# Second layer of a one-core decoder kernel: other exchange of block halves, a shared product in its own output bank, v read from PSUM

## The chip, the cores and the metric

The kernel runs on one core of one Trainium2 chip. The metric is the device time of one execution in microseconds; several executions are taken and the median is given. The profile is of one further execution of the same program.

## The reference, cut to what matters

The decoder has three parts on an input of 16 x 256 x 512 float32: a state-space layer, a gated long convolution along the last axis, and a feed-forward layer with low-rank experts. Each ends in a layer norm with a residual. The change concerns the second part, for head h (32 heads of 8 channels):

```
kv  = v[b,h,i,:] * x2[b,h,j,:]              # all 8 x 8 pairs of channels, 512 positions
y   = causal convolution of kv with k[h]     # the reference uses an FFT of twice the length
y   = y + kv * skip
out[b,h,j,:] = sum over i of y[..i,j,:] * x1[b,h,i,:]
x   = layernorm(x + out)
```

`v` is the output of the first layer; `x1` and `x2` are both the context tensor. The feed-forward part (`base = x @ W.T`, gates from the top two of eight logits, low-rank update) runs in the same loop over heads, one head late.

## The kernel before, in words

The first layer takes the first 757 us of the span. After it comes the loop over 32 heads (line 1198 on). In a head the 512 positions are four blocks of 128, so a Toeplitz matrix of k[h] acts on each pair of blocks (`lb` out, `mb` in). Lag matrices `T` are prepared on the host and loaded by `load_T` into the same buffer as `kv` (two buffers). The 16 batches are two halves, `q` = 0 and 1; in each half `kv` of a block is 128 positions x 512 columns.

For one half of one head the kernel does the following.

- **Products (`products`, L158, VectorE):** `kv` of half q, two instructions of 128x1024, from `vT` and `cT`. They are made one head ahead. `vT` is v with positions on partitions: `turned_v` (L146) makes four TensorE transposes into a PSUM tile of tag `tr`, and ScalarE copies that tile to SBUF (L148).
- **Seed (`seeded`, L1002 and L1003):** blocks 2 and 3 need the same lag matrix on blocks 0 and 1, so GpSimd makes `xs`, the sum of the two (`pair_sum`, L979), TensorE multiplies it once into a PSUM bank of its own (`yc`, in pool `ps_b`), and one ScalarE copy of 128x1024 spreads it over both banks of `y[1]`.
- **Convolution (`convolve`, L1014 and L1032):** four full matmuls of 128x128 on 512 columns (two with differences `Td` of lag matrices, made on GpSimd, L984) and twelve matmuls of 64x64 for the triangles on the diagonal, in three groups of four that run side by side on the four quarters of the array. [...]The result lies in `y[0]` and `y[1]`, two PSUM banks each, with one buffer per tag. The order of blocks and the exchange of 64-row halves (`BLOCKS_IN`, `SWAPPED_IN`, `BLOCKS_OUT`, `SWAPPED_OUT`) are chosen so that the four quarters are taken in every group; one of the quadrants (`AGAIN`) needs a copy of half of `kv` on the other partitions, `kvd`, which ScalarE makes (`again`, L994).
- **Contraction (`multiplied` L1067, `reduced` L1077, VectorE):** each of `y[1]`, `y[0]` is multiplied by `cT` and summed over i, in this order, two instructions of each.

After half 0, the GpSimd part (`skip_term`, then `with_residual`, L948 and L950) adds skip term and v into `o`: one 128x128 instruction and two of 64x384 that move data between partition halves. In half 1 of the contraction the head before is finished: `o + red` on GpSimd (L1225), four transposes (L1104, `centre`), gates (`gates`), the feed-forward matmuls (`feed_forward`, L1193, and `lora`, L1189), and the output.

The engines' order is written by hand: program order is the order on each engine, and the tile framework adds only the waits for data and for buffers. In a head h > 0, TensorE's order is: feed-forward block 3 of the head before, transpose `xat`, seed 0, `lora`, four transposes of v (`turned_v`), convolution 0, four transposes of `centre`, seed 1 (inside `meanwhile`), eight passes for `gl`, feed-forward blocks 0 to 2, convolution 1. VectorE's order is: contraction of half 1 of the head before, row sums, products 0 of the next head, contraction of half 0, products 1 of the next head, gates.

[...]two for tag `tr`, one for `yc`, one for `base`, four for `y`.

Of the kernel before, what the change touches and what calls it, by code (L numbers as in the profile page):

```python
# [37 lines left out]
BLOCKS_IN, SWAPPED_IN = (2, 0, 1, 3), (3,)  # L38
BLOCKS_OUT, SWAPPED_OUT = (0, 1, 3, 2), (0, 1)


GIVEN = ((3, 2), (3, 0), (2, 0), (1, 0), (0, 0), (2, 2), (3, 3))
FULL_AT = {(3, 2): 0, (2, 1): 0, (3, 0): 1, (2, 0): 2, (3, 1): 2, (1, 0): 3}
TRIANGLE_AT = (4, 4, 5, 6)
# [3 lines left out]
    (0, 0, 0), (3, 0, 1), (1, 1, 0), (2, 1, 1),  # L48
    (2, 0, 0), (0, 0, 1), (3, 1, 0), (2, 0, 1),
    (1, 0, 0), (1, 0, 1), (0, 1, 0), (3, 1, 1),  # L50
)

AGAIN = (2, 0, 1)
# [18 lines left out]
def decoder_kernel(  # L72
# [48 lines left out]
    def load_T(h):  # L121

        both = big.tile([P, NQ * NL * BQ * NH * NH + len(GIVEN) * P], F32, tag="big", name="kv")
        kv, T = both[:, 0 : NQ * NL * BQ * NH * NH], both[:, NQ * NL * BQ * NH * NH :]
        T = T.rearrange("p (k l) -> p k l", l=P)
        nc.sync.dma_start(T, toep[h])
        return kv.rearrange("p (q k b j i) -> p q (k b) j i", q=NQ, k=NL, j=NH, i=NH), T

    def load_c(h):


        cT = q3.tile([P, NQ, 7, BQ * NH], F32, tag="cT", name="cT")
        nc.sync.dma_start(cT, ctxT[h])
        return cT
# [7 lines left out]
    def turned_v(vn):  # L142

        tr = ps_t.tile([P, NL, P], F32, tag="tr", name="tr")
        for k, blk in enumerate(BLOCKS_IN):
            nc.tensor.transpose(tr[:, k, :], vn[:, blk * P : (blk + 1) * P], ident)  # L146
        vT = q2.tile([P, NQ, NL, BQ * NH], F32, tag="vT", name="vT")
        nc.scalar.copy(  # L148
            vT.rearrange("p q k t -> p k q t"), tr.rearrange("p k (q t) -> p k q t", q=NQ)
        )  # L150
        return vT

    def products(vT, cT, kv, q, ks=(0, NL // 2)):

        full = [P, NL * BQ // 2, NH, NH]
        for k in ks:
            blks = slice(k, k + NL // 2)
            last = nc.vector.tensor_tensor(  # L158
                kv[:, q, k * BQ : (k + NL // 2) * BQ],
                vT[:, q, blks].rearrange("p k (b i) -> p (k b) i", i=NH).unsqueeze(2)  # L160
                .to_broadcast(full),
                cT[:, q, 1 + k : 1 + k + NL // 2].rearrange("p k (b j) -> p (k b) j", j=NH).unsqueeze(3)
                .to_broadcast(full),
                ALU.mult,
            )
        return last
# [14 lines left out]
    with ExitStack() as s1:  # L181
# [361 lines left out]
        for g in range(NG):  # L543
# [307 lines left out]
            else:  # L851
                finish_sums()
                gated(1, spread_heads(1))
                for n, t in enumerate((0, 2, 1, 3)):


                    ps = ps_s.tile([P, 512], F32, tag="s", name="s") if n in (0, 3) else bank()
                    for c in range(NI):
                        for j in range(2):
                            nc.tensor.matmul(  # L860
                                ps[:, j * S : (j + 1) * S],
                                zs[c][:, t * P : (t + 1) * P],
                                w_o[c // HC, j][c % HC],
                                start=(c == 0 and j == 0),
                                stop=(c == NI - 1),
                                skip_group_check=True,
                            )
                        if n == 3 and c == 3:
                            heads["vT"] = turned_v(heads["vn"].pop(0))
                            heads["vn"] = [load_v(1)]  # L870
                    if n == 3:
                        for q in range(NQ):
                            products(heads["vT"], cTs[0], kvs[0][0], q)
                    r = xs[t]
                    nc.vector.scalar_tensor_tensor(r, r, 2.0, ps, ALU.mult, ALU.add)
                    normalised(g, (t, r))
                    if n == 1:
                        heads["vn"] = [load_v(0)]
                        kvs = [load_T(0), load_T(1)]
# [22 lines left out]
    with ExitStack() as s2:  # L902
# [42 lines left out]
        def with_residual(t, vT):  # L945

            o = p2.tile([P, NQ, NL, BQ * NH], F32, tag="o", name="o")
            nc.gpsimd.tensor_tensor(o[:, :, 3], t[:, :, 0], vT[:, :, 0], ALU.add)  # L948
            for a, b in ((0, HP), (HP, 0)):
                nc.gpsimd.tensor_tensor(  # L950
                    o[b : b + HP, :, 0:3],
                    t[a : a + HP, :, 1:4],
                    vT[a : a + HP, :, 1:4],
                    ALU.add,
                )
            return o
# [15 lines left out]
        def prepared(kv, T):  # L972


            xs = p2.tile([P, NQ, BQ * NH * NH], F32, tag="xs", name="xs")
            Td = p2.tile([P, 2, P], F32, tag="Td", name="Td")

            def pair_sum(q):
                return nc.gpsimd.tensor_tensor(  # L979
                    xs[:, q], moving(kv, q, 0), moving(kv, q, 1), ALU.add  # L980
                )

            def differences():
                nc.gpsimd.tensor_tensor(  # L984
                    Td, T[:, 0:2], T[:, 2:3].to_broadcast([P, 2, P]), ALU.subtract
                )

            return xs, Td, pair_sum, differences

        def again(kv):  # L990

            kvd = p2.tile([P, NQ, BQ * NH * NH], F32, tag="kvd", name="kvd")
            for q in range(NQ):
                nc.scalar.copy(kvd[HP:, q], moving(kv, q, 2)[0:HP])  # L994
            return kvd

        def seeded(y, T, xs, q):

            yc = ps_b.tile([P, BQ * NH * NH], F32, tag="yc", name="yc")
            nc.tensor.matmul(yc, T[:, 2, :], xs[:, q], start=True, stop=True)  # L1002
            nc.scalar.copy(y[1], yc.unsqueeze(1).to_broadcast([P, 2, BQ * NH * NH]))  # L1003

        def convolve(y, kv, T, Td, kvd, q, between=None, late=False, early=None, ahead=None):
# [18 lines left out]
            def quadrant(lb, r, c):  # L1024
                start = lb not in begun and (lb, c) not in begun
                begun.add((lb, c))
                src, at = moving(kv, q, lb), TRIANGLE_AT[lb]
                if (lb, r, c) == AGAIN:

                    r, src, at = 1 - r, kvd[:, q], TRIANGLE_AT[3]  # L1030
                rows, cols = slice(r * HP, (r + 1) * HP), slice(c * HP, (c + 1) * HP)
                return nc.tensor.matmul(  # L1032
                    bank_of(y, lb)[cols],
                    T[rows, at, cols],
                    src[rows],
# [29 lines left out]
        def multiplied(y, cT, q, i):  # L1065
# [4 lines left out]
                cT[:, q, 5 - 5 * i : 7 - 5 * i].rearrange("p k (b i) -> p k b i", i=NH)  # L1070
# [88 lines left out]
        vT_next, vns = heads["vT"], heads["vn"]  # L1159
        more_next = prepared(*kvs[0])  # L1160
        kvd_next = again(kvs[0][0])
# [5 lines left out]
        def ahead():  # L1167
            vT_ahead.append(turned_v(vns.pop(0)))
            vns.append(load_v(2))
            cTs.append(load_c(2))  # L1170
# [10 lines left out]
        def turned_gates(xa, at=None):  # L1181
            xat = (at or ps_t).tile([ER, P], F32, tag="yc" if at else "tr", name="xat")
# [15 lines left out]
        for h in range(HX):  # L1198
            nxt, ff = h + 1 < HX, last is not None
            (kv, T), cT, vT = kvs.pop(0), cTs.pop(0), vT_next  # L1200
            (xs, Td, _, _), kvd = more_next, kvd_next
# [5 lines left out]
            if h:  # L1207
                if rest is not None:
                    base, o_r, xa = rest
                    feed_forward(base, o_r, (3,))  # L1210
                    turned = turned_gates(xa)
# [3 lines left out]
                if nxt:  # L1215
                    vT_after = turned_v(vns.pop(0))
                    kvs.append(load_T(h + 1))
                    if h + 2 < HX:
                        vns.append(load_v(h + 2))
                        cTs.append(load_c(h + 2))  # L1220
# [12 lines left out]
            convolve(y, kv, T, Td, kvd, 0, late=h == 0, ahead=ahead)  # L1233
            if h == 0:
                vT_after = vT_ahead[0]
            ws = skip_sum(sk_next)
            behind = None
            if nxt:
                kv_n, T_n = kvs[0]
                cT_n, vT_next = cTs[0], vT_after  # L1240
                if h:
                    behind = products(vT_next, cT_n, kv_n, 0)
# [4 lines left out]
            else:  # L1247

                prs = []
                for i in range(2):  # L1250
                    prs.append(multiplied(y, cT, 0, i))
                    behind = products(vT_next, cT_n, kv_n, 0, (i * NL // 2,))
# [24 lines left out]
            if nxt:  # L1277
                products(vT_next, cT_n, kv_n, 1)
# [7 lines left out]
            if nxt:  # L1286
                convolve(y, kv, T, Td, kvd, 1)
                kvd_next = again(kv_n)
                rest = (base, o_l, xa) if ff else None
            else:  # L1290
# [3 lines left out]
                    y, kv, T, Td, kvd, 1, lambda: lora(base, turned), True,  # L1294
# [9 lines left out]
        gl = ps_b.tile([P, NE + ER], F32, tag="yc", name="gl")  # L1304
        o_l = {}

        def contracted(src, ks):
# [4 lines left out]
            cs = 5 if ks[0] < 2 else -2  # L1312
# [26 lines left out]
        def norms_and_gates(*ks):  # L1339
            for k in ks:  # L1340
                nc.tensor.transpose(tr[:, k, :], own(k), ident)
            for k in ks:
                nc.tensor.matmul(
                    gl, own(k), w_gl[:, k, :], start=(k == 0), stop=(k == 2),
# [12 lines left out]
        contracted(y_f[2].unsqueeze(1), (3,))  # L1357
        contracted(y_f[1][:, 0:1, :], (2,))
        norms_and_gates(0, 1)
        feed(0)  # L1360
        norms_and_gates(3, 2)
        for k in (1, 3, 2):
            feed(k)
# [84 lines left out]
```

## Time and profile before

| what | value |
|---|---|
| median of 3 runs | 1430.14 us (1429.83 to 1431.35) |
| span of the profiled execution | 1429.6 us |
| granted TensorE clock, mean | 0.999 |
| TensorE busy | 1415.0 us, 99% of the span |
| VectorE busy | 1215.5 us, 85% |
| GpSimd busy | 559.8 us, 39% |
| ScalarE busy | 461.5 us, 32% |
| distance from head to head in the loop | 20.61 us |

The span goes from the first to the last instruction of the core; the profile does not give the time around it. Busy times are unions over instructions of the engine. A line "L1014" is a line of the kernel's source; PE is TensorE's matmul, PEld its weight load, DVE VectorE, ACT ScalarE, POOL GpSimd, SPq the queue that issues DMAs. In a timeline a row is a run of like instructions: start, length, engine, line, operation, output <- inputs, count, and in brackets the idle time before it with what ended it.

### The profile page before, as it was taken

To read this page: it belongs to the slowest core of one execution; us is meant where nothing else is said; L and a number is where in the kernel's file an instruction comes from. 1 tells how busy PE (TensorE), PEld (TensorE's weight loads), DVE (VectorE), ACT (ScalarE), POOL (GpSimd) and SP (SyncE) were. 2 spreads that over 40 slices of the span, in tenths; PEclk is the share of its full clock that TensorE was granted. 3 is DMA by queue.
4 is the path that set the end of the run, shared out by engine and by line. 5 is a ranking of instruction groups with operands and counts; after the bars stand their busy time and mean duration, and the time that the engine had idled before them with its cause. 6 is when DMAs were issued, how large, how long until landed. Compare 5 with 4: busy or idle time off the path is not lost.

```text
span 1429.6 us, 19152 instructions
## 1 busy us (share of the span) xinstructions
PE 1415.0 (99%) x6956; PEld 913.5 (64%) x6956; DVE 1215.5 (85%) x2102; ACT 461.5 (32%) x964; POOL 559.8 (39%) x655
## 2 busy tenths in 40 slices
PE   8999999999999999999999999999999999999997
PEld 7888788787888888888884444444444444444443
DVE  6988778877888787877848999999999999999996
ACT  2423323233232332322312333333333333333331
POOL 5450010100100201001004776677677767766772
PEclk9999999999999999999999999999999999999999
DMA  8014021120121201212003212221221222122200
GB/s 300 33 38 131 16 75 46 38 83 8 56 68 42 74 17 39 83 45 88 15 18 114 71 53 81 74 67 64 82 74 61 69 74 81 60 70 74 80 30 23
DMA packets 49167, 93.38 MB, mean 65 GB/s; under 512 B 8880, under 2 KB 13360, under 8 KB 49072
## 3 DMA queue, kind: packets, MB, share of 16 engines
q1 hardware_dynamic: 49072, 92.15, 20.0%
q8 instruction: 55, 0.90, 0.3%
q14 instruction: 40, 0.33, 0.1%
HBM read 74.82 MB, written 17.32 MB: 64 GB/s over the span
## 4 chain that ended last, share of the span: by engine, by line
PE 96%; DVE 1%; issue 1%; POOL 1%; DMA 0%; SPq 0%; POOLq 0%; ACT 0%; DVEq 0%; ACTq 0%
PE mm L329 20%; PE y L1014 15%; PE s L329 14%; PE y L1032 12%; PE base L1193 8%; PE s L769 6%; PE mm L769 6%; PE yc L1002 4%; PE gl L1270 2%; PE base L1189 2%; PE tr L1104 1%; PE mm L726 1%; PE xm L589 1%; PE mm L860 1%; PE tr L146 1%
## 5 line engine op out<-in xcount | busy, mean ns | idle before, releaser
L1067 DVE TENSOR_TENSOR pr<-y,cT 128x1024 f32<-128x1024 f32 x126 | 148.4, 1219 | 40.4 <-PE y L1032 37.2
L158 DVE TENSOR_TENSOR kv<-vT,cT 128x1024 f32<-128x1024 f32 x128 | 179.4, 1442 | 1.5 <-ACT vT L148 1.5
L1032 PE MATMUL y<-kv 64*64 64x512 f32 x1408 | 179.7, 598 | 0.0
L578 DVE SCALAR_TENSOR_TENSOR acc<-xi,wc,acc 128x512 f32<-128x512 f32 x192 | 142.3, 754 | 7.4 <-ACT acc L574 1.7
L1077 DVE TENSOR_REDUCE red<-pr 128x128 f32<-128x1024 f32 x126 | 147.1, 1208 | 0.0
L1014 PE MATMUL y<-kv 128*128 128x512 f32 x272 | 127.9, 593 | 1.0 <-ACT y L1003 1.0
L1032 PEld LDWEIGHTS y<-kv 64*64 64x64 f32 x1408 | 51.2, 132 | 119.4 <-issue 91.0
L950 POOL TENSOR_TENSOR o<-t,vT 64x384 f32<-64x384 f32 x64 | 121.9, 1905 | 4.4
L1193 PE MATMUL base<-w_f,ol 128*128 128x512 f32 x248 | 119.5, 605 | 0.0
L1014 PE MATMUL y<-kv,Td 128*128 128x512 f32 x248 | 116.5, 592 | 0.0
L67 POOL TENSOR_TENSOR rs_a<-ve_a,nhalf 128x1 f32<-128x1 f32 x32 | 19.0, 594 | 243.1 <-DVE ve_a L65 243.1
L390 POOL TENSOR_TENSOR rstd<-ms,nhalf 128x4 f32<-128x4 f32 (+1 forms) x9 | 8.5, 947 | 260.6 <-DVE ms L388 260.6
L329 PE MATMUL mm<-XT,w_z 128*128 128x256 f32 x384 | 90.7, 379 | 0.0
L1014 PEld LDWEIGHTS y<-kv,Td 128*128 128x128 f32 x248 | 47.1, 190 | 59.3 <-issue 59.3
L979 POOL TENSOR_TENSOR xs<-kv 128x512 f32<-128x512 f32 x63 | 81.3, 1290 | 2.4
L1014 PEld LDWEIGHTS y<-kv 128*128 128x128 f32 x272 | 48.9, 190 | 51.9 <-issue 48.7
L329 PEld LDWEIGHTS mm<-XT,w_z 128*128 128x128 f32 x384 | 73.0, 190 | 9.9
L1193 PEld LDWEIGHTS base<-w_f,ol 128*128 128x128 f32 x248 | 42.3, 189 | 54.5 <-issue 54.5
L1003 ACT COPY y<-yc 128x1024 f32<-128x1024 f32 x62 | 61.8, 997 | 32.9 <-PE yc L1002 23.9
L329 PE MATMUL mm<-xnT,w_z 128*128 128x256 f32 x288 | 71.0, 382 | 0.0
L1225 POOL TENSOR_TENSOR ol<-o,red 128x512 f32<-128x512 f32 x31 | 39.4, 1271 | 79.3 <-DVE red L1077 79.1
L1032 PE MATMUL y<-kvd,kv 64*64 64x512 f32 x128 | 65.2, 589 | 0.0
(278 smaller groups left out, 2940.3 us busy)
## 6 DMA issues: line engine op xcount, KB each, us to landing
cT<-in_ctxT SPq DMA_DIRECT2D x32, 448.0 KB
kv<-in_toep SPq DMA_DIRECT2D x32, 448.0 KB
xt<-in_x SPq DMA_DIRECT2D x32, 256.0 KB
spread<-both SPq DMA_DIRECT2D x32, 256.0 KB
first<-xt SPq DMA_DIRECT2D x32, 256.0 KB
vn<-first SPq DMA_DIRECT2D x32, 256.0 KB
out<-res SPq DMA_DIRECT2D x31, 256.0 KB
xnT<-in_xT SPq DMA_DIRECT2D x7, 1024.0 KB
```

What stands on the lines that cost most here:

```text
L158: last = nc.vector.tensor_tensor(kv[:, q, k * BQ : (k + NL // 2) * BQ], vT[:, q, blks].rearrange("p k (b i) -> p (k b) i", i=NH).unsqueeze ...
L329: nc.tensor.matmul(ps, w[:, p, a, kc, :], Xs[b][:, kc, :], start=start and kc == 0, stop=stop and kc == 1, skip_group_check=upon,)
L578: ins = nc.vector.scalar_tensor_tensor(acc, xi[:, :, k : k + S], wc[:, c, k : k + 1], acc, ALU.mult, ALU.add)
L769: nc.tensor.matmul(ps, own[a][c][:, n * P : (n + 1) * P], w_o[b][c], start=start and c == 0, stop=stop and c == HC - 1, skip_group_check=upon,
L950: nc.gpsimd.tensor_tensor(o[b : b + HP, :, 0:3], t[a : a + HP, :, 1:4], vT[a : a + HP, :, 1:4], ALU.add,)
L979: return nc.gpsimd.tensor_tensor(xs[:, q], moving(kv, q, 0), moving(kv, q, 1), ALU.add)
L1003: nc.scalar.copy(y[1], yc.unsqueeze(1).to_broadcast([P, 2, BQ * NH * NH]))
L1014: nc.tensor.matmul(bank_of(y, lb), w, moving(kv, q, mb), start=not late and lb not in begun, stop=False, skip_group_check=True,)
L1032: return nc.tensor.matmul(bank_of(y, lb)[cols], T[rows, at, cols], src[rows], start=start, stop=False, skip_group_check=True,)
L1067: nc.vector.tensor_tensor(pr.rearrange("p (k b j) i -> p k b j i", k=2, j=NH), y[i].rearrange("p k (b j i) -> p k b j i", j=NH, i=NH), cT[ ...
L1077: nc.vector.tensor_reduce(red[:, q, 2 * i : 2 * i + 2, :].rearrange("p k t -> p (k t)"), pr, AX.X, ALU.add)
L1193: nc.tensor.matmul(base, o_l[:, kc, :], w_f[:, kc, :], start=(first and kc == kcs[0]), stop=False)
```

## The change

Only the second layer is touched.

- The order of blocks and the exchanged halves are others: in (0, 1, 3, 2) with 2 and 3 exchanged, out (1, 0, 2, 3) with 1 and 2 exchanged. With these, all twelve quadrants take `kv` where it lies; `kvd` and its two ScalarE copies a head go. The same number of full matmuls and quadrants is issued.
- `seeded` multiplies straight into the bank of block 3, the second bank of `y[1]`, and two ScalarE copies of 64x512 bring it, halves exchanged, to the bank of block 2. The bank `yc` goes; its place in `ps_b` is a tile of tag `vp`.
- `turned_v` writes the transposes of v to `vp`, already in the order of `vT`. `products` read v from this PSUM tile, and each waits for ScalarE's copy to `vT` as well; `vT` is still made for `with_residual`. In the loop the block with `turned_v`, `load_T`, `load_v` and `load_c` is moved to the head's beginning, ahead of feed-forward block 3, `xat` and the seed.
- `with_residual` takes the two middle blocks and the two outer ones apart: one GpSimd instruction of 128x256 on aligned partitions and two of 64x256 that change halves.
- The host makes six lag matrices and six context blocks a head instead of seven each.

```diff
-BLOCKS_IN, SWAPPED_IN = (2, 0, 1, 3), (3,)
-BLOCKS_OUT, SWAPPED_OUT = (0, 1, 3, 2), (0, 1)
+BLOCKS_IN, SWAPPED_IN = (0, 1, 3, 2), (2, 3)
+BLOCKS_OUT, SWAPPED_OUT = (1, 0, 2, 3), (1, 2)
...
-    def turned_v(vn):
+    def turned_v(vn, pool, tag):
...
-        tr = ps_t.tile([P, NL, P], F32, tag="tr", name="tr")
+        tr = pool.tile([P, NQ, NL, BQ * NH], F32, tag=tag, name="tr")
...
-        return vT
+        kept = nc.scalar.copy(vT, tr)
+        return vT, tr, kept
...
+            if kept is not None:
+                wait_for(last, kept)
...
-            nc.gpsimd.tensor_tensor(o[:, :, 3], t[:, :, 0], vT[:, :, 0], ALU.add)
+            straight, turned = slice(1, 3), slice(0, NL, NL - 1)
+            nc.gpsimd.tensor_tensor(
+                o[:, :, straight], t[:, :, turned], vT[:, :, turned], ALU.add
+            )
             for a, b in ((0, HP), (HP, 0)):
                 nc.gpsimd.tensor_tensor(
-                    o[b : b + HP, :, 0:3],
-                    t[a : a + HP, :, 1:4],
-                    vT[a : a + HP, :, 1:4],
+                    o[b : b + HP, :, turned],
+                    t[a : a + HP, :, straight],
+                    vT[a : a + HP, :, straight],
...
-        def again(kv):
-
-            kvd = p2.tile([P, NQ, BQ * NH * NH], F32, tag="kvd", name="kvd")
-            for q in range(NQ):
-                nc.scalar.copy(kvd[HP:, q], moving(kv, q, 2)[0:HP])
-            return kvd
...
-            yc = ps_b.tile([P, BQ * NH * NH], F32, tag="yc", name="yc")
-            nc.tensor.matmul(yc, T[:, 2, :], xs[:, q], start=True, stop=True)
-            nc.scalar.copy(y[1], yc.unsqueeze(1).to_broadcast([P, 2, BQ * NH * NH]))
+            yc = bank_of(y, 3)
+            nc.tensor.matmul(yc, T[:, SHARED_AT, :], xs[:, q], start=True, stop=True)
+            for a, b in ((0, HP), (HP, 0)):
+                nc.scalar.copy(bank_of(y, 2)[b : b + HP], yc[a : a + HP])
...
             if h:
+                if nxt:
+                    v_after = turned_v(vns.pop(0), ps_b, "vp")
+                    kvs.append(load_T(h + 1))
+                    if h + 2 < HX:
+                        vns.append(load_v(h + 2))
+                        cTs.append(load_c(h + 2))
                 if rest is not None:
...
-                if nxt:
-                    vT_after = turned_v(vns.pop(0))
-                    kvs.append(load_T(h + 1))
-                    if h + 2 < HX:
-                        vns.append(load_v(h + 2))
-                        cTs.append(load_c(h + 2))
...
-                products(vT_next, cT_n, kv_n, 1)
+                products(v_n, cT_n, kv_n, 1)
...
-                convolve(y, kv, T, Td, kvd, 1)
-                kvd_next = again(kv_n)
+                convolve(y, kv, T, Td, 1)
```

## The prediction on record

> **What bounds the kernel now.** I read the page's busy times and chain first, then the sums over the loop of heads (800 to 1400 us), then one head's timeline on TensorE, VectorE and ScalarE, and the waits last.
>
> ```profile
> PE 1415.0 (99%) x6956; PEld 913.5 (64%) x6956; DVE 1215.5 (85%) x2102; ACT 461.5 (32%) x964; POOL 559.8 (39%) x655
> PE 96%; DVE 1%; issue 1%; POOL 1%; DMA 0%; SPq 0%; POOLq 0%; ACT 0%; DVEq 0%; ACTq 0%
> 800.00:1400.00 600.00, 600.00 (x2767) 259.32 (x2769) 554.85 (x726) 216.56 (x466) 418.22 (x468) 1.00 0.21 68
> ```
>
> The third line is the sums: of 600 us PE is busy 600.00 and DVE 554.85. In the timelines (1000 to 1045 us for PE, 1000 to 1024 for DVE and ACT) no PE row carries an idle time:
>
> ```profile
> 1009.12 1.04 PE L1032 MATMUL y<-kv 64*64 64x512 f32 x8
> 1010.08 0.66 PE L1104 MATMUL tr<-ident,ol 128*128 128x128 f32 x4
> 1010.58 1.02 PE L1002 MATMUL yc<-xs,kv 128*128 128x512 f32 x2
> 1011.44 1.09 PE L1270 MATMUL gl<-w_gl,ol 128*128 128x136 f32 x8
> ...
> 1021.20 1.12 PE L1193 MATMUL base<-w_f,ol 128*128 128x512 f32 x2
> 1022.16 0.27 PE L1183 MATMUL xat<-ident,xa 128*128 128x128 f32 x1
> 1022.27 1.02 PE L1002 MATMUL yc<-xs,kv 128*128 128x512 f32 x2
> 1023.13 1.02 PE L1189 MATMUL base<-w_lb,xaT 128*128 128x512 f32 x2
> 1023.99 0.60 PE L146 MATMUL tr<-ident,vn 128*128 128x128 f32 x4
> 1024.43 1.88 PE L1014 MATMUL y<-kv 128*128 128x512 f32 x4
> ```
>
> ```profile
> 1010.25 2.35 DVE L1067 TENSOR_TENSOR pr<-y,cT 128x1024 f32<-128x1024 f32 x2 [1.26 <-PE y L1032]
> ...
> 1021.37 2.35 DVE L1067 TENSOR_TENSOR pr<-y,cT 128x1024 f32<-128x1024 f32 x2
> ```
>
> ```profile
> 1011.68 1.00 ACT L1003 COPY y<-yc 128x1024 f32<-128x1024 f32 x1 [0.16 <-PE yc L1002]
> ```
>
> Passes of 512 columns follow each other every 0.43 us; heads follow every 20.61 us (v's transposes at 1003.38 and 1023.99). DVE waits for PE at half 0's contraction (1.26 us here). So PE sets the time, and a head gets longer by what PE is made to wait and by nothing else. What matters in these rows: the seed (L1002) is what PE does between a convolution and its next work while DVE is still reading the finished `y`. It may do so because its output `yc` is a bank of its own. Only ACT's copy has to wait for DVE.
>
> [...]So a seed written into `y[1]` has to wait for DVE's last read of it. The trace agrees as far as it can: ACT's copy into `y[1]` never overlaps that read (1011.68, after 1011.47).
> [...]POOL's one-column nm_c (L1090) averages 1177 ns where nm_b, the same operation elsewhere, takes 223; the product of 128x1024 averages 1441 ns, and `pr<-y,cT` of equal size, with y in PSUM, 1219.
> [...]Here a gap of 1.36 us left passes at 0.43 us; I count no loss of clock.
>
> **The change, part by part (one head).**
>
> *PE's work:* full matmuls, seeds and the twelve quadrants are as many as before. Each new group of four still takes four different quarters of the array. 0.
>
> *Seed 1, the step that decides.* Convolution 0 ends at 1010.15 (last pass 1009.56 plus 0.59). DVE's first multiplication, that of `y[1]`, starts at 1010.25 and takes 1.22: it ends at 1011.47. From DVE's end to a PE weight load that waited for it the tail shows 0.11 us (xa ends 1421.39, xat's load 1421.505). So seed 1 can begin at 1011.58 in place of 1010.58: 1.01 us. A matmul that waited also starts without its weights loaded ahead: two passes after a wait span 1.13 where others span 1.02 (below), 0.11 more. Together **1.11 us**. Queued behind it on PE are `gl`, three feed-forward blocks and convolution 1, nothing that could go first; the transposes of `centre` are already ahead of it. 30 heads (1 to 30) have it: 30 x 1.11 = **33.4 us**.
>
> *Seed 0 and the moved block.* v's four transposes come first now, so the new order after convolution 1 is: transposes 1021.20 to 1021.69 (as L1104: 0.16, then 0.11 each), feed-forward block 3 to 1022.55, xat to 1022.66, seed. DVE ends with `y[1]` at 1021.37 + 1.22 = 1022.59, plus 0.11 makes 1022.70. The wait is 0.04, the load 0.11: **0.15 us**, in heads 2 to 30: 4.4 us. The moved transposes are thus cover for the seed; without them it would stand 0.43 + 0.11. Head 31 has none to move: 0.5 us. Of what moves with them, SP's three DMAs (T, v, c) are issued sooner; `load_c` must wait until DVE has read the context of the head before (to 1023.7), and behind it on SP is nothing before the output's store, ten us on. `load_T` waits for the end of the convolution as before. ACT makes `vT` ahead of `xaT`, in time that it spends waiting: xaT is ready at about 1023.1, `lora` wants it at 1023.5. The bank `vp` was last read by products 1, which end at 1017.9; it's free. No cost.
>
> *The seed's copies.* Before: one of 997 ns. After: two of 64x512. No row shows that form from PSUM; the nearest are 586 ns (vT, 128x512 from PSUM) and 614 (kvd, 64x512 from SBUF). I take two of 0.59 with starts 0.53 apart, 1.12 us. At seed 0 they run from 1023.91 to 1025.03, and full matmul (3,2), first to need them, loads its weights at about 1025.0 to 1025.2, behind `lora` and full (1,0). It just fits: 0, with bounds of 0 and 0.3 us (9 us in all). At seed 1 there are over 3 us to spare.
>
> *ACT:* kvd's copies (2 x 614 ns) go; ACT is busy 36% in the loop, and its copies end before anything waits. 0. In half 1 the squares for `rs_b` start 1.3 us later, behind the copies; `rs_b` is then ready at about 1015.6, and DVE wants it at 1017.2. Hidden.
>
> *DVE and POOL:* products 1 overlap POOL's `o` and took 3.15 us for two where products 0 took 2.44. Reading v from PSUM should make all four 1.22: 0.7 to 0.9 us a head. The added wait for `kept` ends at about 1022.6, four us before products 0 start. POOL's `o` of 0.46 + 3.96 becomes about 2.1 (64x384 takes 1.03 uncontended in the last head, so 0.7 for 64x256 and for 128x256). Both engines gain one to two us a head, and neither is on the path: the gain becomes longer waits for PE, so 0. If DVE were slower at v from PSUM, it would have to lose over 2 us a head to be felt.
>
> *DMA:* 64 KB less of T and of context a head, landed long before use. 0.
>
> *Entry of the loop:* two waits stand there (timeline from 738 to 790 us):
>
> ```profile
> 768.70 1.13 PE L1014 MATMUL y<-kv 128*128 128x512 f32 x2 [0.99 <-ACT y L1003]
> ...
> 775.64 1.12 PE L1002 MATMUL yc<-xs,kv 128*128 128x512 f32 x2 [1.36 <-POOL xs L979]
> ```
>
> In head 0, `y[1]` is read at 766.33 to 767.54, so seed 1 runs from 767.66 to 768.62 and (3,2) starts when its copies end, at 770.06 in place of 768.70: +1.4. In head 1 POOL is early enough, so that wait goes, and the seed's own wait and its copies take its place, as `lora` is not there to cover them: about +0.1 more. Sum **1.5 us**. kvd's copies at the entry delayed no PE row. The tail has the same work in another order of blocks: 0.
>
> **Sum.** 33.4 + 4.4 + 0.5 + 1.5 = 39.8 us on a span of 1429.6: 1469.4. The median shown is 0.5 above this span; I take that for what lies around it, and forecast 1470 us, a head of 21.87 us. About 0.2% (3 us) is what a measurement here can tell from no change.
>
> **The rivals.**
>
> *A, the copies are late as well (slower still).* If (3,2) waits at seed 0, up to 0.3 us x 31 heads come on top: 1479. For it: the margin is 0.1 to 0.2 us. Against: ACT is otherwise idle there.
>
> *B, smaller waits.* If weights load ahead in spite of the wait, the two seeds cost 1.01 and 0.04, together 31.5, and the sum is 33 to 34: 1463.
>
> *C, no visible wait: 1430 to 1432.* The seed would have to be kept from waiting, for example because DVE ended its read within PE's transposes (0.5 us). It takes 1.22 us and starts only when PE has ended.
>
> *D, faster: the relief of DVE and POOL decides.* Products give 0.8 us a head, [...]about 1406 if only the products count. It decides from the point where DVE is what PE waits for. For it: DVE is busy 92% of the loop. Against: DVE waits for PE in every head (36 us in 29 waits), PE never for it.
>
> **How the numbers follow.** The forecast with A and B holds 0.94: slower. C gets 0.03, D 0.03. The range goes from below B's sum, for a start of the seed some 0.1 us earlier than I have it, to A's end: 1459 to 1479.
>
> **What would show it.** Right: heads 21.8 to 22.0 us apart; PE busy still near 1415 us but 96% of the span; the seed at half 1 with an idle time of about 1 us ended by DVE `pr` in each of 30 heads, with passes that span 1.13; almost none at half 0. Products at 1.22 us, nm_c near 0.22, two copies of about 0.59, and DVE's wait for PE at half 0 grown by 1 to 3 us. Wrong: seeds without idle time, heads of 20.6 us, or a head longer by waits of L1014 for ACT.

## The result, and the profile after

The changed kernel takes 1461.26 us (median of 4 runs, 1461.14 to 1462.02) where the kernel before takes 1430.39 (4 runs, 1429.83 to 1431.35): a ratio of 1.0217, 95% interval 1.0203 to 1.023. It is slower by 30.9 us. The span of the profiled execution grew from 1429.6 to 1459.5 us; the measured time of that execution is 1461.27, so 1.8 us lie around the span.

Busy times of the page and the sums over 800 to 1400 us, in the same columns as before:

```profile
PE 1423.8 (98%) x6956; PEld 915.1 (63%) x6956; DVE 1185.4 (81%) x2102; ACT 438.1 (30%) x962; POOL 462.4 (32%) x655
PE 94%; DVE 4%; issue 1%; POOL 1%; DMA 0%; ACT 0%; POOLq 0%; SPq 0%; DVEq 0%; ACTq 0%
```

```profile
800.00:1400.00 600.00, 579.65 (x2647) 248.48 (x2645) 503.21 (x697) 187.02 (x444) 312.93 (x448) 1.00 0.19 61
```

In this window all the other columns fell, in part because fewer heads fit into it. Over the whole span VectorE lost 30 us of work, GpSimd 97 and ScalarE 23, and TensorE issues the same 6956 matmul passes (one matmul of a seed is two of them, x2 in its row, and the four of `gl` are x8; four transposes are x4). But in the loop TensorE is now busy 579.65 of 600 us where it was busy in all 600, and the chain that ended last has 4% on VectorE where it had 1%. One head on TensorE, with the rows that answer to those shown before:

```profile
1008.77 2.81 PE L1025 MATMUL y<-kv 64*64 64x512 f32 x24
1011.51 0.66 PE L145 MATMUL tr<-ident,vn 128*128 128x128 f32 x4
1012.00 1.02 PE L1185 MATMUL base<-w_f,ol 128*128 128x512 f32 x2
1012.86 0.27 PE L1175 MATMUL xat<-ident,xa 128*128 128x128 f32 x1
1012.97 1.06 PE L997 MATMUL y<-xs,kv 128*128 128x512 f32 x2
...
1018.26 2.81 PE L1025 MATMUL y<-kv 64*64 64x512 f32 x24
1020.99 0.66 PE L1097 MATMUL tr<-ident,ol 128*128 128x128 f32 x4
1022.38 1.12 PE L997 MATMUL y<-xs,kv 128*128 128x512 f32 x2 [0.72 <-DVE pr L1060]
1023.34 1.09 PE L1262 MATMUL gl<-w_gl,ol 128*128 128x136 f32 x8
...
1030.37 2.81 PE L1025 MATMUL y<-kv 64*64 64x512 f32 x24
```

Only one row of the head has an idle time: seed 1 (L997), ended by VectorE's `pr`. The bracket gives 0.72 us, which counts from the modelled end of the last transpose; in the flow of the transposes, one every 0.11 us, the seed would have begun at 1021.49, so 0.89 us are lost there, and its pair of passes spans 1.12 in place of 1.02, 0.1 more. What VectorE did at that time:

```profile
1021.10 2.36 DVE L1060 TENSOR_TENSOR pr<-y,cT 128x1024 f32<-128x1024 f32 x2 [1.35 <-PE y L1025]
```

It was itself waiting for TensorE's convolution, then read `y[1]` for 1.22 us, to 1022.32. The seed's weight load starts 0.05 us later. So the two engines hand the same bank to each other: at this point of the head VectorE waits for TensorE's convolution, and then TensorE for VectorE's read.

A measure without any modelled end is the distance from the first quadrant (L1032 before, L1025 after) of one convolution to that of the next. In the rows above it is 1018.26 - 1008.77 = 9.49 us and 1030.37 - 1018.26 = 12.11. In the kernel before, the same rows are

```profile
1007.35 1.51 PE L1032 MATMUL y<-kv 64*64 64x512 f32 x11
1018.47 1.51 PE L1032 MATMUL y<-kv 64*64 64x512 f32 x11
1027.96 1.51 PE L1032 MATMUL y<-kv 64*64 64x512 f32 x11
```

with 11.12 and 9.49 us between them. The table of these distances is what the rest of this document uses:

| from | to | before | after | difference |
|---|---|---|---|---|
| half 0 | half 1 of the same head, heads 1 to 30 | 11.12 | 12.11 | +0.99, 30 times (one of those before is 11.27) |
| half 1 | half 0 of the next head, to heads 2 to 30 | 9.49 | 9.49 | 0.00 |
| head 0, half 0 | half 1 | 14.05 | 15.41 | +1.36 |
| head 0, half 1 | head 1, half 0 | 9.15 | 9.28 | +0.13 |
| head 30, half 1 | head 31, half 0 | 9.05 | 9.49 | +0.44 |
| first to last convolution, all | | 648.9 | 680.2 | +31.3 |

The tail behind is 23.2 us in both. What comes before the first convolution was 757.42 us in the profile before and 756.02 after; in this case's ten profiles it lies between 755.85 and 757.48 whichever kernel runs, so its 1.4 us belong to the execution.

### The profile page after: what moved, and what is told of

It is laid out like the page before. It is cut to its first block, busy times and chain, and to the rows that moved or that the text cites. A ratio compares the mean times of both kernels' runs of the same rounds, so it can differ in the third digit from the quotient of the medians.

```text
span 1459.5 us, 19028 instructions
## 1 busy us (share of the span) xinstructions
PE 1423.8 (98%) x6956; PEld 915.1 (63%) x6956; DVE 1185.4 (81%) x2102; ACT 438.1 (30%) x962; POOL 462.4 (32%) x655
## 4 chain that ended last, share of the span: by engine, by line
PE 94%; DVE 4%; issue 1%; POOL 1%; DMA 0%; ACT 0%; POOLq 0%; SPq 0%; DVEq 0%; ACTq 0%
PE mm L328 20%; PE y L1010 15%; PE s L328 13%; PE y L1025 12%; PE base L1185 7%; PE s L768 6%; PE mm L768 6%; PE y L997 4%; DVE pr L1060 3%; PE gl L1262 2%; PE base L1181 2%; PE tr L145 1%; PE mm L725 1%; PE xm L588 1%; PE mm L859 1%
## 5 line engine op out<-in xcount | busy, mean ns | idle before, releaser
L1025 PE MATMUL y<-kv 64*64 64x512 f32 x1536 | 179.6, 598 | 0.0
L155 DVE TENSOR_TENSOR kv<-tr,cT 128x1024 f32<-128x1024 f32 x124 | 145.5, 1215 | 0.0
L1025 PEld LDWEIGHTS y<-kv 64*64 64x64 f32 x1536 | 52.2, 132 | 119.0 <-issue 96.8
L1185 PE MATMUL base<-w_f,ol 128*128 128x512 f32 x248 | 116.5, 593 | 0.0
L997 PE MATMUL y<-xs,kv 128*128 128x512 f32 x124 | 67.9, 629 | 24.5 <-DVE pr L1060 23.5
L999 ACT COPY y<-y 64x512 f32<-64x512 f32 x124 | 69.2, 558 | 65.1 <-PE y L997 63.1
L1185 PEld LDWEIGHTS base<-w_f,ol 128*128 128x128 f32 x248 | 42.5, 190 | 30.9 <-issue 30.9
L328 PE MATMUL s<-XT,w_xi 128*128 128x256 f32 x256 | 61.0, 380 | 0.9 <-DVE XT L224 0.6
```

Of the source, the lines that this page charges most:

```text
L155: last = nc.vector.tensor_tensor(kv[:, q, k * BQ : (k + NL // 2) * BQ], vT[:, q, blks].rearrange("p k (b i) -> p (k b) i", i=NH).unsqueeze ...
L328: nc.tensor.matmul(ps, w[:, p, a, kc, :], Xs[b][:, kc, :], start=start and kc == 0, stop=stop and kc == 1, skip_group_check=upon,)
L997: nc.tensor.matmul(yc, T[:, SHARED_AT, :], xs[:, q], start=True, stop=True)
L999: nc.scalar.copy(bank_of(y, 2)[b : b + HP], yc[a : a + HP])
L1025: return nc.tensor.matmul(bank_of(y, lb)[cols], T[rows, DIAGONAL_AT, (b - a) * HP : (b - a + 1) * HP], moving(kv, q, lb)[rows], start=star ...
L1185: nc.tensor.matmul(base, o_l[:, kc, :], w_f[:, kc, :], start=(first and kc == kcs[0]), stop=False)
```

## The experiments

All are the changed kernel with one thing altered, or more where it is said. Three explanations were set against each other. **S**: TensorE waits at seed 1 for VectorE's read of `y[1]`. **V**: v in PSUM, with the products' added wait, costs the time. **C**: the two ScalarE copies hold up full matmul (3,2).

**Seed 1 moved behind other work (`seed_later`).**

```diff
                 if nxt and not ff:      # inside meanwhile: head 0 alone
                     seeded(y, T, xs, 1)
...
-                feed_forward(base, o_l, (0, 1, 2) if nxt else (0, 1, 2, 3), True)
+                feed_forward(base, o_l, (0,), True)
+                if nxt:
+                    seeded(y, T, xs, 1)
+                feed_forward(base, o_l, (1, 2) if nxt else (1, 2, 3))
```

> The changed kernel with seed 1 moved behind the eight gl passes and the first feed-forward block on TensorE, in heads 1 to 30; nothing else. Theory S (TensorE waits at seed 1 for VectorE's read of y[1]): the gl passes and one block take 0.93 + 0.86 us, more than the 0.99 us a head that the convolution starts show, so the wait goes and heads come 20.6 us apart again: 1461.3 - 30 x 0.99 = 1431.6 us, 1430 to 1433. Rival V (v in PSUM, with the products' added wait): no effect, 1461. Rival C (the two ScalarE copies hold up full matmul (3,2)): the copies come 1.8 us later, so no gain or slower, 1461 to 1475.

Measured: 1431.7 us (21 runs), 1.0011 of the kernel before (1.0004 to 1.0017). Half 0 to half 1 takes 11.12 us again. The rows have no idle time left:

```profile
1010.08 0.66 PE L1097 MATMUL tr<-ident,ol 128*128 128x128 f32 x4
1010.57 1.09 PE L1262 MATMUL gl<-w_gl,ol 128*128 128x136 f32 x8
1011.50 1.02 PE L1185 MATMUL base<-w_f,ol 128*128 128x512 f32 x2
1012.36 1.02 PE L997 MATMUL y<-xs,kv 128*128 128x512 f32 x2
1013.21 1.88 PE L1185 MATMUL base<-w_f,ol 128*128 128x512 f32 x4
1014.93 1.88 PE L1010 MATMUL y<-kv 128*128 128x512 f32 x4
```

Everything else of the change is in this kernel: v from PSUM, two copies, other halves. So these cost nothing that shows in the loop, and S accounts for all but about 1.5 us. What is left stands where the table has it: head 0 (15.40), head 1 (9.27), head 31 (9.48).

**Seed 1 behind half of gl (`seed_mid`).** The seed stands between the second and the third of the four `gl` matmuls:

```diff
                 for kc in range(KD):
+                    if kc == 2 and nxt:
+                        seeded(y, T, xs, 1)
```

> The changed kernel with seed 1 between the second and third of the four gl matmuls: four gl passes (0.46 us) ahead of it. Theory S: the wait shrinks by just that, from 0.99 to 0.53 us a head (half 0 to half 1 takes 11.65 us in place of 12.11): 1461.3 - 30 x 0.46 = 1447.4 us. If the delay belonged to the seed's place in itself and not to the end of VectorE's read, it would be 1461 or 1431.

Measured: 1447.49 us, half 0 to half 1 in 11.65 us. The delay shrinks by 0.46 us a head, which is the work put ahead of the seed; its row says 0.26 us where it said 0.72:

```profile
1017.63 1.13 PE L997 MATMUL y<-xs,kv 128*128 128x512 f32 x2 [0.26 <-DVE pr L1060]
```

**VectorE reads y[0] first (`order_01`).** The same instructions on each engine, two of VectorE's exchanged:

```diff
-                contract(y, cT, red, 0, (1, 0))
+                contract(y, cT, red, 0, (0, 1))
```

> The changed kernel with the contraction of half 0 in the order y[0], y[1], in heads 1 to 31: VectorE's read of y[1] ends one multiplication later (they start 1.14 us apart). The same instructions on every engine. Theory S: the wait at seed 1 grows by 1.14 us in 30 heads, 34 us: 1495 us, heads of 22.7. Rivals V and C: seed and copies have their cover from gl and the feed-forward blocks, 1461 to 1463.

Measured: 1529.44 us, 1.0697 of before (1.0682 to 1.0712). The direction is that of S, V and C are out, but it is 34 us more than S foresaw. The distances show why: half 0 to half 1 takes 13.36 us in some heads (S: 13.25) and 15.03 in others. Sums over two seeds of this kernel, from one of each kind, and the rows of the first; the column after the busy times is the granted clock:

```profile
999.50:1004.30 4.80, 3.42 (x10) 2.42 (x11) 4.80 (x6) 1.38 (x5) 1.25 (x2) 0.64 0.01 3
1022.70:1027.30 4.60, 2.59 (x19) 1.90 (x16) 4.43 (x4) 1.45 (x4) 1.25 (x2) 1.00 0.00 0
```

```profile
1000.88 2.04 PE L997 MATMUL y<-xs,kv 128*128 128x512 f32 x2 [2.01 <-DVE pr L1060]
1002.71 1.84 PE L1262 MATMUL gl<-w_gl,ol 128*128 128x136 f32 x8
```

In the first, two seed passes span 2.04 us and eight gl passes 1.84, where they span 1.10 and 1.09 in the second:

```profile
1025.37 1.10 PE L997 MATMUL y<-xs,kv 128*128 128x512 f32 x2 [2.01 <-DVE pr L1060]
1026.31 1.09 PE L1262 MATMUL gl<-w_gl,ol 128*128 128x136 f32 x8
```

The granted clock averaged 0.64 over the first stretch and 1.00 over the second, and from the seed's first pass to gl's first it took 1.83 us in place of 0.94, about twice as long. It was so in 18 of the 30 heads, which is 18 x 1.68 = 30.2 us (15.04 against 13.36); the 1.68 us at half the clock make some 3.4 us of lowered clock a time, an estimate. With 30 x 1.25 = 37.5 us for the longer wait (13.36 against 12.11) the sum is 67.7 us; measured are 68.2 more than the changed kernel. The wait is 0.11 us longer than S had it. Of this 0.06 is VectorE's start: it now reads first the banks whose quadrants come last, and begins 0.093 us after TensorE's last pass in place of 0.034. The other 0.05 lies between VectorE's end and the seed's second pass.

**The same with a shorter gap (`order_01_mid`).** Both edits, contraction order and seed behind half of gl.

> The order y[0], y[1] in the contraction of half 0 together with seed 1 behind four gl passes: TensorE's gap there is about 1.7 us in place of 2.2. With the gap of 2.2 us the clock was halved for 3.4 us in 18 heads, 1.7 us each. Theory S alone: half 0 to half 1 takes 13.36 - 0.46 = 12.90 us in every head, 1461.3 + 30 x 0.79 = 1485 us. If a gap of 1.7 us still halves the clock in some heads: up to 30 us more, 1515.

Measured: 1485.23 us, 12.90 us in every head, and the clock, 0.999 in the mean of the span, shows no loss in the loop of heads. The row says 1.54 where it said 2.01:

```profile
1010.32 1.10 PE L997 MATMUL y<-xs,kv 128*128 128x512 f32 x2 [1.54 <-DVE pr L1060]
```

So S gives the size in three strengths of wait, 0.53, 0.99 and 1.78 us a head, as soon as the clock stays up.

**v from SBUF (`v_from_sbuf`).**

```diff
-                products(v_n, cT_n, kv_n, 1)
+                products(vT_next, cT_n, kv_n, 1)
```

and the same for products 0, without the wait for `kept`.

> The changed kernel with products that read vT from SBUF as before and have no extra wait; the transposes still go to the bank vp, the seed still to y[1]. Theory S: the time stays within 2 us of 1461[...]. Rival V: back to 1430 to 1435.

Measured: 1461.65 us, 1.0218 of before. V is out. One figure was a miss: the author's estimate for the products was 1.4 us, and they average 1239 ns. Groups by shape of this kernel (busy time, mean ns), then those of the changed kernel:

```profile
L155 DVE TENSOR_TENSOR kv<-vT,cT 128x1024 f32<-128x1024 f32 x112 | 134.5, 1239 | 0.0
L1083 POOL TENSOR_SCALAR nm_c<-sum_c 128x1 f32<-128x1 f32 x28 | 33.9, 1211 | 0.0
L948 POOL TENSOR_TENSOR o<-t,vT 128x256 f32<-128x256 f32 x28 | 36.8, 1313 | 0.0
```

```profile
L155 DVE TENSOR_TENSOR kv<-tr,cT 128x1024 f32<-128x1024 f32 x112 | 131.4, 1215 | 0.0
L1083 POOL TENSOR_SCALAR nm_c<-sum_c 128x1 f32<-128x1 f32 x28 | 6.6, 236 | 0.0
L948 POOL TENSOR_TENSOR o<-t,vT 128x256 f32<-128x256 f32 x28 | 20.3, 725 | 0.0
```

Among what takes longer with v in SBUF are two of GpSimd's instructions: `nm_c`, 1211 ns in place of 236 (1177 in the kernel before), and `o` of 128x256, 1313 ns in place of 725. VectorE's products, 1441 ns in the kernel before, take 1239 in place of 1215. None of it reaches the time.

**Seed in a bank of its own (`own_bank`).**

```diff
-            yc = bank_of(y, 3)
+            yc = ps_b.tile([P, BQ * NH * NH], F32, tag="vp", name="yc")
...
+            nc.scalar.copy(bank_of(y, 3), yc)
```

with v's transposes in tag `tr` and products from `vT`, which the bank requires. Products from `vT` alone cost nothing, as the run before shows.

> The changed kernel with the seed in a bank of its own again (tag vp), spread by three ScalarE copies (128x512 and two of 64x512); for the bank, v's transposes go back to tag tr and products read vT from SBUF. The exchange of halves, the missing kvd, the residual and the moved block stay. Theory S: seed 1 waits for nothing, heads of 20.6 us, 1430 to 1433 us. Rival V: also near 1431, so this one speaks against C alone. Rival C: three copies are 0.6 us more than two, so slower than 1461.

Measured: 1440.91 us, 1.0074 of before (1.006 to 1.0088). Half 0 to half 1 takes 11.12 us: seed 1 waits for nothing, as S says. The other 10 us are a cost that none of the expectations had: half 1 to half 0 takes 9.84 in place of 9.49. The third copy is late for (3,2):

```profile
1005.51 0.57 ACT L998 COPY y<-yc 128x512 f32<-128x512 f32 x1 [0.59 <-PE yc L997]
1006.12 1.15 ACT L1000 COPY y<-yc 64x512 f32<-64x512 f32 x2
```

```profile
1006.17 2.27 PE L1011 MATMUL y<-kv 128*128 128x512 f32 x4
```

The four full passes take 2.27 us in place of 1.88, since (3,2) stands until the copies end at 1007.27. One copy of 0.61 us costs 0.35, so with two copies some 0.26 us were to spare. So the wait of C exists, and the changed kernel lies just short of it: there the weights of (3,2) already load only when the copies end (at 1015.22), but its passes are not late.

```profile
1015.27 0.51 PEld L1010 LDWEIGHTS y<-kv 128*128 128x128 f32 x2 [0.35 <-ACT y L999]
```

**The moved block put back (`block_back`).** v's transposes and the three loads stand behind `lora` again.

> The changed kernel with v's transposes and the loads of T, v and c behind lora again, where they stood before the change. Theory S: seed 0 loses its cover, as in head 31 of the changed kernel, where half 1 to half 0 takes 9.49 in place of 9.05 us without transposes: 0.44 us in 29 heads (9.93 in place of 9.49), 12.8 us: 1474 us. If moving the block had been neutral: 1461.

Measured: 1474.04 us, half 1 to half 0 in 9.92 us. Without the transposes in front, seed 0 waits as well:

```profile
1016.04 1.13 PE L1185 MATMUL base<-w_f,ol 128*128 128x512 f32 x2
1017.48 1.10 PE L997 MATMUL y<-xs,kv 128*128 128x512 f32 x2 [0.20 <-issue]
```

The row does not name the wait's cause. The rows of VectorE and of the weight load do:

```profile
1016.15 2.35 DVE L1060 TENSOR_TENSOR pr<-y,cT 128x1024 f32<-128x1024 f32 x2 [1.86 <-PE y L1025]
1017.44 0.30 PEld L997 LDWEIGHTS y<-xs,kv 128*128 128x128 f32 x2 [0.72 <-issue]
```

The first of the two multiplications ends at 1017.37, and the seed's weights load 0.07 us later; this distance is the same in every head of the loop. So moving the block is worth 12.8 us to a kernel whose seed needs `y[1]`.

**The last quadrants in the old order (`quad_last`).**

```diff
-    (3, 1, 1), (2, 1, 1), (1, 1, 1), (0, 1, 1),
+    (1, 1, 1), (0, 1, 1), (3, 1, 1), (2, 1, 1),
```

> The changed kernel with the last group of four quadrants issued in the order block 1, 0, 3, 2 in place of 3, 2, 1, 0, so that those of y[1] come last as before the change. The change let VectorE begin 0.03 to 0.05 us after TensorE's last pass in place of 0.09. If the quadrant's place in the group is the reason: VectorE begins about 0.05 us later, seed 1 too: 12.16 in place of 12.11 us, 1.5 us in all, 1462 to 1464. If not: 12.11.

Measured: 1464.22 us, half 0 to half 1 in 12.155 us in place of 12.11, half 1 to half 0 in 9.53 in place of 9.49. VectorE starts 0.08 us after the last pass in place of 0.034. Together 30 x 0.05 + 30 x 0.04 = 2.7 us, and 3.0 are measured. The expectation had left out the same delay behind half 1, and so the result lies just above its 1462 to 1464.

## Why the prediction was right, point by point

The forecast was 1470 us in a range of 1459 to 1479, slower with a chance of 0.94; 1461.26 was measured. The mechanism held, and the time was put 8.7 us too long (39.8 us of growth were forecast, 30.9 measured). The result lies 2.3 us above the range's lower end, which allowed for a start of the seed some 0.1 us earlier than the sum had it.

- **What bounds the kernel:** held. The relief, one us of VectorE's work and three of GpSimd's a head (30 and 97 us in all), gave nothing, as the kernel with the moved seed shows: it has all the relief and lies 0.11% above the kernel before.
- **Seed 1, 1.11 us in 30 heads:** right in kind and place, sized 0.12 too large (0.99 measured). Two latencies were put too long, the first as it was in the kernel before, the second from another pair of instructions. VectorE starts 0.034 us after the last pass, not 0.093, because the change also made `y[1]`'s quadrants the first of the last group; of these 0.059 us `quad_last` gives 0.046 back. And the seed's load starts 0.05 us after VectorE's end, not 0.11. 30 x 0.12 = 3.6 us. The wait, 0.72 us in its row, is one for data: a seed written earlier would have overwritten sums that VectorE had not read.
- **Seed 0, 0.15 us in 29 heads:** measured 0.00. Its weights load at 1012.91, in time for the flow, so only 0.04 us is lost at its second pass, and 0.05 is won at the first instruction after the quadrants: the first of v's transposes is followed by the next after 0.164 us where the others follow after 0.109, 0.055 more, and the first pass of feed-forward block 3 was followed after 0.533 in place of 0.429, 0.104 more. The sum had no line for this exchange. It makes 4.4 us; with the 3.6 of seed 1 this is 8.0 of the 8.7. The remark that the moved transposes are its cover, worth 0.43 us and more, is what `block_back` measured.
- **Entry and head 31:** predicted 1.5 and 0.5 us, measured 1.49 and 0.44.
- **The copies (rival A):** two of 558 ns each, 0.59 apart; they just fit, as was said. The margin was put at 0.1 to 0.2 us, `own_bank` shows 0.26. Rival A did not occur.
- **Rival B, 1463:** the nearest number, but for another reason: the weights of seed 1 did load late (passes of 1.12), and the smaller sum came from the latencies.
- **Rival C:** seed 1 can't be without a wait where it stands. **Rival D:** refuted with the first point; its price for the products came true (1.215 us) and bought nothing; the comparison of 128x64 (L1122, L1115 after), whose shortening was an estimate of the author's, averages 1282 ns after and 1289 before.
- **What would show it:** heads of 21.60 us, not 21.8 to 22.0, and busy 1423.8 us, not 1415, since of the 0.99 us that a head loses the row of seed 1 shows only 0.72 as idle: 30 x 0.27 = 8.1 us count as busy. The idle rows are where they were said to be. VectorE's wait for TensorE at half 0 was to grow by 1 to 3 us; it went from 1.26 to 1.35, and a second wait, of 1.87 us, appeared at half 1 (before the multiplication at 1011.61).
- **Time around the span:** taken as 0.5 us, it is 1.8 in the profiled run after and in runs of the kernel before (1430.31 us with a span of 1428.5). This moves nothing, since both kernels have it.
- **Slips in figures:** 30 x 1.11 is 33.3, not 33.4; from 1010.58 to 1011.58 is 1.00 us, not 1.01. Neither matters to the sum.

## What to carry to other kernels

A scratch bank that looks like a needless copy can be what lets the bounding engine run ahead of a reader. Before writing straight into the final buffer, look at what the bounding engine does between its last write to that buffer and the next one, and add it up against the reader's time: here 0.5 us of transposes against 1.2 us of reading. If the direct write is wanted, move other work of the same engine in between (gl and one feed-forward block, 30 us), and check that what follows the write, the copies, still fits before its first use. Letting VectorE read block 3's bank in an instruction of its own, to see whether it comes free sooner, was not tried.

## What the runs showed of the hardware

In `order_01` TensorE's clock was lowered to about half (1.83 us in place of 0.94 from seed to gl) for some 3.4 us (the estimate above) after 18 of the 30 gaps ahead of seed 1, in `order_01_mid` after none; the mean granted clock of the span is 0.978 in the one and 0.999 in the other. The rows give the gaps as 2.01 and 1.54 us (the expectation counts 2.2 and 1.7, from where the next pass would have started). The gap alone does not settle it: the two seeds of `order_01` shown above have the same 2.01 us ahead of them, and the clock behind them averaged 0.64 and 1.00. What decides between such heads was not shown, since no run moved a gap in time and kept its length.

The place of a quadrant in a group of four that run side by side (24 passes of quadrants span 2.81 us, four of full matmuls 1.88) mattered to its reader here: VectorE starts 0.034 us after the last pass when the later of its two quadrants is the second of the four, and 0.080 when it is the last (`quad_last`), 0.046 more. It is 0.093 in `order_01`, where VectorE reads `y[0]`, whose quadrants come last.
